# Half of the adjacency tiles built, the other half fetched as transposes

## The chip, the core and the metric

The kernel runs on one core of a Trainium2 chip. The core has a matrix engine (TensorE, PE in the profile; its weight loads are the row PEld), a vector engine (VectorE, DVE), an activation engine (ScalarE, ACT), a general engine (GpSimd, POOL) and a queue engine that issues transfers (SyncE, SP). ACT and POOL issue transfers too. All transfers of the core run on 16 DMA engines. The metric is device time in microseconds of one execution; lower is better.

## The reference, cut to what matters

A graph of N = 6250 nodes with 256 features has E = 106,250 directed edges: 50,000 drawn pairs in both directions and one loop for each node. The layer normalizes the features, runs two graph convolutions, adds a linear attention mix, and ends with a mixture of eight experts of which each node takes two. What the change touches is the aggregation inside the graph convolution:

```python
src = jnp.concatenate([edges[:, 0], edges[:, 1]])
dst = jnp.concatenate([edges[:, 1], edges[:, 0]])
deg = jax.ops.segment_sum(jnp.ones_like(dst, dtype=x.dtype), dst, num_segments=N_NODES)
deg = jnp.maximum(deg, 1.0)
agg = jax.ops.segment_sum(x[src], dst, num_segments=N_NODES) / deg[:, None]
return x @ W0 + b0 + agg @ W1 + b1
```

Every edge is taken in both directions, so the matrix A with agg = A x (before the division by the degree) is symmetric: A[u, v] counts the edges between u and v.

## The kernel before

The nodes are cut into NB = 49 blocks of P = 128. A is cut into 49 x 49 blocks of 128 x 128. The kernel treats T = 4 block columns at once as a group g; there are NGRP = 13 groups, the last one block wide. A *step* (g, j) handles the tile of A whose rows are block j and whose columns are the four blocks of group g: 128 x 512 elements, in bf16 128 KB. There are 13 x 49 = 637 steps, 49 of them narrow (128 x 128).

The kernel has five stages. The first (to about 383 us) normalizes the nodes and sorts edges into slots. The second, `aggregate` (the first graph pass, 383 to 1154 us), runs over all steps. The third, dense, stage (1154 to 1555 us) computes the first layer's output and the second layer's input. The fourth (the second graph pass, 1555 to 2192 us) multiplies by A again, and runs routing work (`gate`) of each finished group beside it. The fifth runs the experts.

A step of the first pass has these parts. `one_hots` (L649) compares slot numbers with a counter on DVE. `adjacency` multiplies two one-hot matrices for each of the blocks (L668), which gives the counts in PSUM, and copies them with ACT to a float tile `adj` (L671); the same instruction sums each row, which gives the degrees (`degp`). `keep` converts the tile to bf16 on DVE (L679) and stores it to DRAM (`adjd`, L680) from SP's queue. `products` multiplies (L626): the features of block j, split into a high and a low part (`sent`, k = 0 and 1), for two halves of the features (c), four matmuls of 512 columns, and adds into the two PSUM tiles `sum0` and `sum1` of the group over all j. The loop of `aggregate` runs these three out of step: comparisons for step t, building for step t - 1, storing and products for step t - 3. The order on PE, DVE and ACT is as written; in the first pass SP's is the scheduler's, which put stores in order of steps. `kept` and `adj` have four buffers each.

In the second pass `reload` (L808) reads seven steps' tiles in one transfer, with two buffers of seven steps; `widen` converts a tile from bf16 to float, by turns on ACT (L946) and DVE (L948), four steps ahead of `products`. The dense stage already issues the first two reloads. The scheduler decides SP's order in the second pass; the gate's load of `bt` (L956) is issued there too. Some expert weights are loaded from POOL's queue at the start of the second pass (L1093, L1095).

The dense stage's weights (`W0_0`, `W1_0`, `W0_1`, `W1_1`, 512 KB each) are loaded from POOL's queue ahead of the first pass (L608) and stay in memory through it.

`aggregate_any` is another way to compute the same, taken only where the edges don't fit the slots; here it is skipped.

Of the kernel before, what the change touches and what calls it, by code (L numbers as in the profile page):

```python
# [8 lines left out]
F32 = mybir.dt.float32  # L9
F32R = mybir.dt.float32r  # L10
BF16 = mybir.dt.bfloat16
I32 = mybir.dt.int32
AF = mybir.ActivationFunctionType
OP = mybir.AluOpType
AX = mybir.AxisListType
ENG = mybir.EngineType
PSUM = bass.MemoryType.PSUM
DRAM = bass.MemoryType.DRAM
P = 128

T = 4
# [18 lines left out]
def tile_gps_layer(ctx: ExitStack, tc: tile.TileContext, a, out):  # L40
    nc = tc.nc
# [9 lines left out]
    NB = -(-(N + 1) // P)  # L51
    NGRP = -(-NB // T)
# [14 lines left out]
    def blocks(g):  # L67
        return range(g * T, min(NB, g * T + T))
# [21 lines left out]
    adjd = dram.tile([NGRP, P, NB, T * P], BF16, name="adjd")  # L90
# [43 lines left out]
    with ExitStack() as p1:  # L134
# [153 lines left out]
        facts, hots, ranks = {}, {}, {}  # L288
# [284 lines left out]
        for b in range(NBAT):  # L573
            ahead_ = count(b + 1) if b + 1 < NBAT else iter(())
            k = b // (PK // PB) + 1
# [26 lines left out]
    wpool_ctx = tc.tile_pool(name="wgnn", bufs=1)  # L602
    wpool = wpool_ctx.__enter__()
    weights = {}
    for name in ("W0_0", "W1_0", "W0_1", "W1_1"):
        k, f = a[name].shape
        weights[name] = wpool.tile([P, k // P, f], F32, name="w" + name)
        nc.gpsimd.dma_start(weights[name], a[name].rearrange("(c p) f -> p c f", p=P))  # L608
    bh2 = wpool.tile([P, 2, FC], F32, name="bh2")
    nc.gpsimd.dma_start(bh2, a["bh"])  # L610
    bh = wpool.tile([P, FC], F32, name="bh")
# [4 lines left out]
    aggT = apool.tile([P, DC, NB * P], F32, name="aggT")  # L616
    degp = apool.tile([P, NB, NGRP], F32, name="degp")

    def products(pg, sums, adj, g, j):

        n = len(blocks(g))
        if j == 0:
            sums[g] = [pg.tile([P, T * P], F32, name=f"sum{c}") for c in range(DC)]
        for c in range(DC):
            for k in range(2):
                nc.tensor.matmul(sums[g][c][:, :n * P], sent[:, j, k, c * P:(c + 1) * P],  # L626
                                 adj[:, :n * P], start=(j == 0 and k == 0),
                                 stop=(j == NB - 1 and k == 1))

    steps = [(g, j) for g in range(NGRP) for j in range(NB)]  # L630

    def aggregate():

        with ExitStack() as s:
            hp = s.enter_context(tc.tile_pool(name="hots", bufs=4))
            ap = s.enter_context(tc.tile_pool(name="adj", bufs=4))
            pa = s.enter_context(tc.tile_pool(name="pa", bufs=4, space=PSUM))
            pg = s.enter_context(tc.tile_pool(name="pg", bufs=2, space=PSUM))
            s.enter_context(tc.manual_schedule(engines={ENG.PE, ENG.DVE, ENG.Activation}))
            hots, adjs, sums = {}, {}, {}  # L640

            def one_hots(t):
                g, j = steps[t]
                bs = blocks(g)
                n = len(bs)

                def compared(m, v0):
                    oh = hp.tile([P, m, P, 2], BF16, name=f"oh{m}")
                    nc.vector.tensor_tensor(  # L649
                        oh, iota2[:, None].to_broadcast([P, m, P, 2]),  # L650
                        place[:, j, v0:v0 + m, None, :].to_broadcast([P, m, P, 2]), op=OP.is_equal)
                    return oh

                hots[t] = (compared(n, bs[0]), compared(1, NB) if j in bs else None)

            def adjacency(t):
                g, j = steps[t]
                n = len(blocks(g))
                pt = pa.tile([P, T * P], F32, name="pt")
                oh, rest = hots.pop(t)  # L660
                for k, i in enumerate(blocks(g)):
                    cols = pt[:, k * P:(k + 1) * P]
                    if i == j:
                        todo = [(o, r) for o in (oh[:, k], rest[:, 0]) for r in range(2)]
                    else:
                        todo = [(oh[:, k], int(j > i))]
                    for m, (o, r) in enumerate(todo):
                        nc.tensor.matmul(cols, o[:, :, r], o[:, :, 1 - r], start=(m == 0),  # L668
                                         stop=(m + 1 == len(todo)))
                adj = ap.tile([P, T * P], F32R, name="adj")  # L670
                nc.scalar.activation(adj[:, :n * P], pt[:, :n * P], AF.Copy,  # L671
                                     accum_out=degp[:, j, g:g + 1])
                adjs[t] = adj

            def keep(t):
                g, j = steps[t]
                n = len(blocks(g))
                kept = ap.tile([P, T * P], BF16, name="kept")
                nc.vector.tensor_copy(kept[:, :n * P], adjs[t][:, :n * P].bitcast(F32))  # L679
                nc.sync.dma_start(adjd[g, :, j, :n * P], kept[:, :n * P])  # L680

            AH, AB = 3, 2
            for t in range(len(steps) + AH):
                if t < len(steps):
                    one_hots(t)
                if 0 <= t - AH + AB < len(steps):
                    adjacency(t - AH + AB)
                if t >= AH:
                    g, j = steps[t - AH]
                    keep(t - AH)  # L690
                    products(pg, sums, adjs.pop(t - AH), g, j)
                    if j == NB - 1:
                        n = len(blocks(g))
                        cols = slice(g * T * P, (g * T + n) * P)
                        nc.vector.tensor_copy(aggT[:, 0, cols], sums[g][0][:, :n * P])
                        nc.scalar.copy(aggT[:, 1, cols], sums[g][1][:, :n * P])

    def aggregate_any(first_conv):
# [3 lines left out]
        with tc.If(nc.values_load(misfit[0:1, 0:1], min_val=0, max_val=1) == 1), ExitStack() as s:  # L702
# [89 lines left out]
            if not first_conv:  # L792
                nc.vector.memset(rdeg, 0.0)

    aggregate()
    nc.vector.tensor_reduce(deg, degp, AX.X, OP.add)
    aggregate_any(True)
    ppool_ctx.__exit__(None, None, None)
    JL = 7
    lp_ctx = tc.tile_pool(name="reload", bufs=2, side="right")  # L800
    lp = lp_ctx.__enter__()
    loaded = {}

    def reload(t):
        g, j = steps[t]
        n = len(blocks(g))
        many = lp.tile([P, JL, T * P], BF16, name="many")
        nc.sync.dma_start(many[:, :, :n * P], adjd[g, :, j:j + JL, :n * P])  # L808
        loaded[g, j] = many


    with ExitStack() as p2:
# [4 lines left out]
        w = weights  # L817
        loads = {}

        def load_group(g):  # L820
            bs = blocks(g)
            cols = slice(bs[0] * P, (bs[-1] + 1) * P)
            xnT = wk.tile([P, DC, T * P], F32, name="xnT2")
            nc.sync.dma_start(xnT[:, :, :len(bs) * P], xnT_d[:, :, cols])
            loads[g] = xnT

        load_group(0)

        nc.vector.tensor_scalar(rdeg, deg, 1.0, None, op0=OP.max)
        nc.vector.reciprocal(rdeg, rdeg)  # L830
# [6 lines left out]
        for g in range(NGRP):  # L837
            bs = blocks(g)
            n = len(bs)
# [23 lines left out]
            for i, b in enumerate(bs):  # L863
                ts = slice(i * P, (i + 1) * P)
                pb = py.tile([P, 512], F32, name="pb")
                for c in range(DC):
                    nc.tensor.matmul(pb[:, :D], xnT[:, c, ts], wmix[:, c, :],
                                     start=(c == 0), stop=False)
                for f in range(FC):
                    nc.tensor.matmul(pb[:, :D], hT[f][:, ts], w["W0_1"][:, f, :], start=False,  # L870
                                     stop=(f == FC - 1))
                nc.vector.tensor_add(bt[:, i], bt[:, i], pb[:, :D])  # L872
                pz = py.tile([P, 512], F32, name="pz")
                for f in range(FC):
                    nc.tensor.matmul(pz[:, :D], hT[f][:, ts], w["W1_1"][:, f, :], start=(f == 0),
                                     stop=(f == FC - 1))
# [1 line left out]
                nc.vector.tensor_sub(sent[:, b, 1], pz[:, :D], sent[:, b, 0].bitcast(F32))  # L878
            nc.sync.dma_start(btab[cols, :].rearrange("(t p) d -> p t d", p=P), bt[:, :n])
            if g == 1:  # L880
                for t in range(0, 2 * JL, JL):
                    reload(t)

    apool_ctx.__exit__(None, None, None)
# [16 lines left out]
    first = gc.tile([P, T, NE], F32, name="first")  # L901
# [29 lines left out]
    with ExitStack() as p3:  # L931
        wk = p3.enter_context(tc.tile_pool(name="work3", bufs=2))
        ap = p3.enter_context(tc.tile_pool(name="adj2", bufs=5))
        pg = p3.enter_context(tc.tile_pool(name="pg2", bufs=2, space=PSUM))
# [3 lines left out]
        adjs, sums = {}, {}  # L938

        def widen(t):  # L940
            g, j = steps[t]
            n = len(blocks(g))
            adj = ap.tile([P, T * P], F32R, name="adj2")
            from_ = loaded[g, j - j % JL][:, j % JL, :n * P]
            if t % 2:
                nc.scalar.copy(adj[:, :n * P], from_)  # L946
            else:
                nc.vector.tensor_copy(adj[:, :n * P], from_)  # L948
            adjs[t] = adj
# [147 lines left out]
        AH = 4  # L1097
        running = iter(())
        for t in range(len(steps) + AH):
            if t < len(steps):  # L1100
                if steps[t][1] % JL == 0 and steps[t] not in loaded:
                    reload(t)
                widen(t)
            next(running, None)
            if t >= AH:
                g, j = steps[t - AH]
                products(pg, sums, adjs.pop(t - AH), g, j)
                if j == NB - 1:
                    for _ in running:
                        pass  # L1110
                    running = gate(g)
# [8 lines left out]
        for e in range(NE):  # L1120
# [35 lines left out]
                         stop=True)  # L1156
# [13 lines left out]
    with ExitStack() as p4:  # L1170
# [5 lines left out]
            engines={ENG.PE, ENG.DVE, ENG.Activation, ENG.SP, ENG.Pool}))  # L1176
# [147 lines left out]
```

## Time and profile before

| | |
|---|---|
| time, median of 3 runs | 2677.56 us (2676.61 to 2684.45) |
| the profiled execution's own time | 2674.58 us |
| its span, first to last instruction | 2672.8 us |
| granted TensorE clock, mean | 0.939 of full speed |
| first pass, busy | PE 768.9 of 771 us, DVE 633.7, ACT 428.3 |
| second pass, busy | PE 631.6 of 637 us, DVE 263.3, ACT 238.8 |
| SP's stores of tiles, L680 | 637, median 320 ns to issue each |

A profile row of the instruction groups names the line, the engine, the operation, the tile written and the tiles read, then the shapes and the count; then the busy time. In the timeline a row is: start, length, engine, line, operation, tiles; in brackets the idle time of that engine just before and what ended it. PE's matmuls overlap, so a step's length is read from one start to the next. A stretch row gives the busy time of each engine in that stretch, then the clock granted to TensorE, the mean busy share of the 16 DMA engines and their rate. The chain that ended last lies almost wholly in the experts' stage and says little of the passes; these are read from the stretches.

### The profile page before, as it was taken

How to read it: one execution, taken by the hardware profiler on the slowest of the kernel's cores; microseconds unless marked ns; L12 is line 12 of the kernel's file. 1: busy time of each engine (PE TensorE's matmuls, PEld its weight loads, DVE VectorE, ACT ScalarE, POOL GpSimd, SP SyncE). 2: the span in 40 equal slices, each digit the busy share in tenths (PEclk: the TensorE clock that was granted, in tenths of full speed). 3: DMA queues.
4: the chain of work that ended last, by engine and by line, in shares of the span. 5: the costliest groups of instructions: out<-in, count | busy, mean ns of one | idle time of the engine just before them, and what ended most of it. 6: DMA issues, size and time to landing. Idle time of an engine off the chain costs nothing. (4 is left out here: it accounts for less than half of the span.)

```text
span 2672.8 us, 41922 instructions
## 1 busy us (share of the span) xinstructions
PE 2452.5 (92%) x13030; PEld 1815.2 (68%) x13030; DVE 1587.8 (59%) x4247; ACT 951.0 (36%) x2476; POOL 344.6 (13%) x375
## 2 busy tenths in 40 slices
PE   3666769999999999989999989999999987999998
PEld 2455547777777777766677768888888874777665
DVE  5999888888888888721111124444434434666665
ACT  1332225555555555511111123334334322323332
POOL 0000000000000000000000011121121122454444
PEclk7777779999999999979999989999999978999999
DMA  2111613333333333222111154445454433223333
GB/s 75 52 51 52 209 54 109 108 107 107 107 107 107 105 110 108 86 66 83 55 56 55 50 208 150 165 161 168 156 166 162 150 120 96 77 76 103 105 112 96
DMA packets 227535, 286.75 MB, mean 107 GB/s; under 512 B 51798, under 2 KB 199937, under 8 KB 227046
## 3 DMA queue, kind: packets, MB, share of 16 engines
q1 hardware_dynamic: 204386, 241.06, 28.1%
q0 software_dynamic: 17072, 34.33, 3.8%
q10 hardware_dynamic: 5844, 8.58, 0.9%
q8 instruction: 107, 1.75, 0.3%
q14 instruction: 126, 1.03, 0.1%
HBM read 151.43 MB, written 147.10 MB: 112 GB/s over the span
## 5 line engine op out<-in xcount | busy, mean ns | idle before, releaser
L626 PE MATMUL sum<-adj,sent 128*128 128x512 f32 (+1 forms) x5096 | 1332.4, 403 | 10.2 <-DVE blank L918 5.9
L626 PEld LDWEIGHTS sum<-adj,sent 128*128 128x128 f32 x5096 | 907.9, 196 | 161.4 <-issue 6.3
L671 ACT ACTIVATE adj<-pt 128x512 fp32r<-128x512 f32 (+1 forms) x637 | 365.7, 574 | 337.2 <-PE pt L668 335.8
L649 DVE TENSOR_TENSOR oh<-iota,place 128x1024 bf16<-128x1024 bf16 (+1 forms) x686 | 426.7, 628 | 0.3 <-PE pt L668 0.2
L679 DVE CAST kept<-adj 128x512 bf16<-128x512 f32 (+1 forms) x637 | 262.1, 411 | 114.9 <-ACT adj L671 106.6
L946 ACT CAST adj<-many 128x512 fp32r<-128x512 bf16 (+1 forms) x318 | 188.8, 595 | 385.9 <-PE sum L626 345.1
L948 DVE CAST adj<-many 128x512 fp32r<-128x512 bf16 (+1 forms) x319 | 135.8, 427 | 318.2 <-PE sum L626 254.8
L668 PE MATMUL pt<-oh 128*128 128x128 bf16 x2548 | 261.5, 224 | 2.4 <-DVE oh L649 1.8
L668 PEld LDWEIGHTS <-oh 128*128 128x128 bf16 x2548 | 151.1, 99 | 161.8 <-DVE oh L649 131.3
L1226 PEld LDWEIGHTS po<-w2e,hT 128*128 128x128 f32 x840 | 159.4, 190 | 67.3 <-issue 26.3
L1206 PE MATMUL pm<-w1e,yT 128*128 x420 | 200.2, 599 | 1.8 <-DMA row<-lists 1.3
L1226 PE MATMUL po<-w2e,hT 128*128 x840 | 198.5, 379 | 1.0 <-ACT hT L1218 1.0
L1230 ACT ACTIVATE res<-res,row 128x256 f32<-128x256 f32 x105 | 53.3, 508 | 301.3 <-DVE res L1229 152.0
L453 PE MATMUL rt<-carry,route 128*128 128x100 bf16 x931 | 81.8, 265 | 84.5 <-DVE carry L440 65.3
L907 POOL IOTA home_i<- 128x8 int32 x1 | 0.1, 128 | 1158.5 <-DVEq L702 1158.5
L453 PEld LDWEIGHTS <-route 128*128 128x128 bf16 x931 | 73.1, 132 | 94.7 <-issue 84.5
L1085 POOL DMA_INDIRECT lists<-rows,place_i x98 | 97.2, 991 | 298.5 <-DVE rows L1077 265.1
L1262 POOL DMA_INDIRECT out_dram<-both,at x105 | 106.0, 1009 | 161.5 <-DVE both L1260 158.7
L872 DVE TENSOR_TENSOR bt<-bt,pb 128x256 f32<-128x256 f32 x49 | 20.6, 421 | 174.1 <-PE pb L870 174.1
L671 ACT ACTIVATION_READ_ACCUMULATOR adj<-pt 128x1 f32 x637 | 123.9, 194 | 0.0
L1247 POOL DMA_INDIRECT got<-ybuf,at x105 | 108.1, 1030 | 84.5 <-issue 33.0
L1209 DVE TENSOR_TENSOR hb<-pm,b1c 128x512 f32<-128x512 f32 x105 | 72.7, 692 | 64.2 <-PE pm L1206 62.0
(253 smaller groups left out, 2557.4 us busy)
## 6 DMA issues: line engine op xcount, KB each, us to landing
adjd<-kept SPq DMA_DIRECT2D x588, 128.0 KB
many<-adjd SPq DMA_DIRECT2D x84, 896.0 KB
row<-lists SPq DMA_DIRECT2D x105, 130.5 KB
ybuf<-xn SPq DMA_DIRECT2D x1, 13440.0 KB
ybuf<-res SPq DMA_DIRECT2D x105, 128.0 KB
xn<-in_x_dram SPq DMA_DIRECT2D x12, 512.0 KB
xnT_d<-xnT ACTq DMA_DIRECT2D x12, 512.0 KB
xnT<-xnT_d SPq DMA_DIRECT2D x12, 512.0 KB
```

The lines of the kernel that those rows point to most:

```text
L453: nc.tensor.matmul(pl[:, r], routes[q // 4][:, q % 4, :, r], carry[:, q - q0, :, :, r], start=(q == 0), stop=(q == Q - 1))
L626: nc.tensor.matmul(sums[g][c][:, :n * P], sent[:, j, k, c * P:(c + 1) * P], adj[:, :n * P], start=(j == 0 and k == 0), stop=(j == NB - 1 a ...
L649: nc.vector.tensor_tensor(oh, iota2[:, None].to_broadcast([P, m, P, 2]), place[:, j, v0:v0 + m, None, :].to_broadcast([P, m, P, 2]), op=OP ...
L668: nc.tensor.matmul(cols, o[:, :, r], o[:, :, 1 - r], start=(m == 0), stop=(m + 1 == len(todo)))
L671: nc.scalar.activation(adj[:, :n * P], pt[:, :n * P], AF.Copy, accum_out=degp[:, j, g:g + 1])
L679: nc.vector.tensor_copy(kept[:, :n * P], adjs[t][:, :n * P].bitcast(F32))
L946: nc.scalar.copy(adj[:, :n * P], from_)
L948: nc.vector.tensor_copy(adj[:, :n * P], from_)
L1206: nc.tensor.matmul(pm, yT[:, c], w1e[:, bass.ds(e, 1), c, :].rearrange("p o f -> p (o f)"), start=(c == 0), stop=(c == DC - 1))
L1226: nc.tensor.matmul(po, hT[:, f], w2e[:, bass.ds(e, 1), f, :].rearrange("p o d -> p (o d)"), start=(f == 0), stop=(f == EC - 1))
L1247: ga = nc.gpsimd.indirect_dma_start(out=gots[t % 4], out_offset=None, in_=ybuf, in_offset=bass.IndirectOffsetOnAxis(ap=outs[t][1][:, 0:1], ...
L1262: st = nc.gpsimd.indirect_dma_start(out=out, out_offset=bass.IndirectOffsetOnAxis(ap=at[:, 1:2], axis=0), in_=both, in_offset=None, bounds ...
```

## The change

Only tiles with j >= 4g (on and below the diagonal in a group's numbering) are built. A tile with j < 4g is "turned": its four blocks are fetched as transposes of blocks that earlier groups stored. For four j at once (j to j + 3, all in group j // 4) and each block i of group g, one transfer on SP's queue reads 128 x 512 elements of bf16, the stored tile of step (j // 4, i), and writes four transposed blocks. So four such transfers (one in the last group) make the tiles of four steps. The steps of a group are put in another order: first the built j from 4g to 48, then the turned ones from 0.

In the first pass a turned step has no comparisons, no building matmuls, no cast and no store; ACT's instruction remains and reads the fetched bf16 tile instead of PSUM. The turned tiles have three buffers of four steps (`turned`), and are asked for eight steps ahead of the products; the one-hot tiles have three buffers instead of four. SP's order is as written there now. In the second pass nothing of the loop's engines changes but the reload: tiles come four steps at a time with three buffers, eight steps ahead, built ones by a plain transfer and turned ones by the transposing transfers, which are made again. The dense stage issues the first two reloads (eight steps). `W0_1` and `W1_1` are loaded at the start of the dense stage from ACT's queue.

```diff
+    def load_weights(pool, queue, *names):
+        for name in names:
+            k, f = a[name].shape
+            weights[name] = pool.tile([P, k // P, f], F32, name="w" + name)
+            queue.dma_start(weights[name], a[name].rearrange("(c p) f -> p c f", p=P))
+
+    load_weights(wpool, nc.gpsimd, "W0_0", "W1_0")
...
-    steps = [(g, j) for g in range(NGRP) for j in range(NB)]
+    steps = [(g, j) for g in range(NGRP) for j in (*range(g * T, NB), *range(g * T))]
+
+    def is_turned(t):
+        g, j = steps[t]
+        return j < g * T
+
+    def ends_of(g):
+
+        return g * T, (g * T - 1) % NB
+
+    def turn_tiles(pool, g, j):
+
+        tl = pool.tile([P, T, T, P], BF16, name="some")
+        for k, i in enumerate(blocks(g)):
+            nc.sync.dma_start(tl[:, :, k, :], adjd[j // T, :, i, :], transpose=True)
+        return tl.rearrange("p j k q -> p j (k q)")
...
-            hp = s.enter_context(tc.tile_pool(name="hots", bufs=4))
+            hp = s.enter_context(tc.tile_pool(name="hots", bufs=3))
             ap = s.enter_context(tc.tile_pool(name="adj", bufs=4))
+            tp_ = s.enter_context(tc.tile_pool(name="turned", bufs=3))
...
-            s.enter_context(tc.manual_schedule(engines={ENG.PE, ENG.DVE, ENG.Activation}))
+            s.enter_context(tc.manual_schedule(engines={ENG.PE, ENG.DVE, ENG.Activation, ENG.SP}))
...
+                adj = ap.tile([P, T * P], F32R, name="adj")
+                adjs[t] = adj
+                if is_turned(t):
+                    nc.scalar.activation(adj[:, :n * P], turned[g, j - j % T][:, j % T, :n * P],
+                                         AF.Copy, accum_out=degp[:, j, g:g + 1])
+                    return
...
-            AH, AB = 3, 2
-            for t in range(len(steps) + AH):
-                if t < len(steps):
+            AT, AH, AB = 8, 3, 2
+            for t in range(AH - AT, len(steps) + AH):
+                if (a_ := t + AT - AH) < len(steps) and is_turned(a_) and steps[a_][1] % T == 0:
+                    turned[steps[a_]] = turn_tiles(tp_, *steps[a_])
+                if 0 <= t < len(steps) and not is_turned(t):
                     one_hots(t)
                 if 0 <= t - AH + AB < len(steps):
                     adjacency(t - AH + AB)
                 if t >= AH:
                     g, j = steps[t - AH]
-                    keep(t - AH)
-                    products(pg, sums, adjs.pop(t - AH), g, j)
-                    if j == NB - 1:
+                    if not is_turned(t - AH):
+                        keep(t - AH)
+                    first, last = ends_of(g)
+                    products(pg, sums, adjs.pop(t - AH), g, j, j == first, j == last)
+                    if j == last:
...
-    JL = 7
-    lp_ctx = tc.tile_pool(name="reload", bufs=2, side="right")
+    lp_ctx = tc.tile_pool(name="reload", bufs=3, side="right")
...
+    AR = 8
...
+        if j % T:
+            return
+        if is_turned(t):
+            loaded[g, j] = turn_tiles(lp, g, j)
+        else:
+            n, m = len(blocks(g)), min(T, NB - j)
+            some = lp.tile([P, T, T, P], BF16, name="some").rearrange("p j k q -> p j (k q)")
+            nc.sync.dma_start(some[:, :m, :n * P], adjd[g, :, j:j + m, :n * P])
+            loaded[g, j] = some
...
         load_group(0)
+        load_weights(p2.enter_context(tc.tile_pool(name="wgnn2", bufs=1)), nc.scalar, "W0_1", "W1_1")
...
-                for t in range(0, 2 * JL, JL):
+                for t in range(AR):
                     reload(t)
...
-                if steps[t][1] % JL == 0 and steps[t] not in loaded:
-                    reload(t)
+                reload(t + AR)
                 widen(t)
```

More of the change, by code (lines that the diff above doesn't have):

```diff
@@ L604, in tile_gps_layer @@
     weights = {}
[L605 to L608, printed above, removed]
+    def load_weights(pool, queue, *names):
[4 more added lines that the diff above has]
+    load_weights(wpool, nc.gpsimd, "W0_0", "W1_0")
     bh2 = wpool.tile([P, 2, FC], F32, name="bh2")
@@ L617, in tile_gps_layer, with products @@
     degp = apool.tile([P, NB, NGRP], F32, name="degp")
-    def products(pg, sums, adj, g, j):
+    def products(pg, sums, adj, g, j, first, last):
         n = len(blocks(g))
-        if j == 0:
+        if first:
             sums[g] = [pg.tile([P, T * P], F32, name=f"sum{c}") for c in range(DC)]
@@ L626, in products @@
                 nc.tensor.matmul(sums[g][c][:, :n * P], sent[:, j, k, c * P:(c + 1) * P],
-                                 adj[:, :n * P], start=(j == 0 and k == 0),
-                                 stop=(j == NB - 1 and k == 1))
-    steps = [(g, j) for g in range(NGRP) for j in range(NB)]
+                                 adj[:, :n * P], start=(first and k == 0),
+                                 stop=(last and k == 1))
+    steps = [(g, j) for g in range(NGRP) for j in (*range(g * T, NB), *range(g * T))]
[9 more added lines that the diff above has]
+        return tl.rearrange("p j k q -> p j (k q)")
     def aggregate():
         with ExitStack() as s:
-            hp = s.enter_context(tc.tile_pool(name="hots", bufs=4))
+            hp = s.enter_context(tc.tile_pool(name="hots", bufs=3))
             ap = s.enter_context(tc.tile_pool(name="adj", bufs=4))
+            tp_ = s.enter_context(tc.tile_pool(name="turned", bufs=3))
             pa = s.enter_context(tc.tile_pool(name="pa", bufs=4, space=PSUM))
             pg = s.enter_context(tc.tile_pool(name="pg", bufs=2, space=PSUM))
-            s.enter_context(tc.manual_schedule(engines={ENG.PE, ENG.DVE, ENG.Activation}))
-            hots, adjs, sums = {}, {}, {}
+            s.enter_context(tc.manual_schedule(engines={ENG.PE, ENG.DVE, ENG.Activation, ENG.SP}))
+            hots, adjs, sums, turned = {}, {}, {}, {}
             def one_hots(t):
@@ L669, in adjacency @@
                                          stop=(m + 1 == len(todo)))
-                adj = ap.tile([P, T * P], F32R, name="adj")
                 nc.scalar.activation(adj[:, :n * P], pt[:, :n * P], AF.Copy,
                                      accum_out=degp[:, j, g:g + 1])
-                adjs[t] = adj
             def keep(t):
@@ L798, in tile_gps_layer @@
     ppool_ctx.__exit__(None, None, None)
-    JL = 7
-    lp_ctx = tc.tile_pool(name="reload", bufs=2, side="right")
+    lp_ctx = tc.tile_pool(name="reload", bufs=3, side="right")
     lp = lp_ctx.__enter__()
     loaded = {}
+    AR = 8
     def reload(t):
+        if t >= len(steps):
+            return
         g, j = steps[t]
[L806 to L809, printed above, removed]
+        if j % T:
+            return
+        if is_turned(t):
[5 more added lines that the diff above has]
+            loaded[g, j] = some
     with ExitStack() as p2:
@@ L943, in widen @@
             adj = ap.tile([P, T * P], F32R, name="adj2")
-            from_ = loaded[g, j - j % JL][:, j % JL, :n * P]
+            from_ = loaded[g, j - j % T][:, j % T, :n * P]
             if t % 2:
@@ L1106, in tile_gps_layer @@
                 g, j = steps[t - AH]
-                products(pg, sums, adjs.pop(t - AH), g, j)
-                if j == NB - 1:
+                first_, last = ends_of(g)
+                products(pg, sums, adjs.pop(t - AH), g, j, j == first_, j == last)
+                if j == last:
                     for _ in running:
```

## The prediction

> **What bounds the kernel now.** The page first, for the totals, then busy time and granted clock by stage, then one step of each graph pass in order of time.
>
> The head of the page and its engine rows:
>
> ```profile
> span 2672.8 us, 41922 instructions
> PE 2452.5 (92%) x13030; PEld 1815.2 (68%) x13030; DVE 1587.8 (59%) x4247; ACT 951.0 (36%) x2476; POOL 344.6 (13%) x375
> ```
>
> Stretches of the trace: first pass, second pass (columns: length, then busy time and count of PE, PEld, DVE, ACT, POOL, then granted clock, DMA share, GB/s):
>
> ```profile
> 383.00:1154.00 771.00, 768.86 (x5095) 558.70 (x5096) 633.71 (x1337) 428.28 (x1288) 4.28 (x6) 0.98 0.32 106
> 1555.00:2192.00 637.00, 631.59 (x2956) 516.11 (x2956) 263.29 (x946) 238.84 (x399) 116.50 (x140) 0.97 0.49 162
> ```
>
> PE is busy from end to end in both, at nearly the full clock; DVE has 137 us free in the first, SP and DMA more. One built step of the first pass:
>
> ```profile
> 702.95 0.40 PE L668 MATMUL pt<-oh 128*128 128x128 bf16 x4
> 703.16 1.17 PE L626 MATMUL sum<-adj,sent 128*128 128x512 f32 x4
> 703.24 0.69 DVE L649 TENSOR_TENSOR oh<-iota,place 128x1024 bf16<-128x1024 bf16 x1
> 703.35 0.32 SPq L680 DMA_DIRECT2D adjd<-kept  x1
> 703.39 0.60 ACT L671 ACTIVATE adj<-pt 128x512 fp32r<-128x512 f32 x1 [0.53 <-PE pt L668]
> 703.88 0.19 ACT L671 ACTIVATION_READ_ACCUMULATOR adj<-pt 128x1 f32 x1
> 704.11 0.43 DVE L679 CAST kept<-adj 128x512 bf16<-128x512 f32 x1 [0.19 <-ACT adj L671]
> 704.17 0.40 PE L668 MATMUL pt<-oh 128*128 128x128 bf16 x4
> ```
>
> The step repeats after 704.17 - 702.95 = 1.22 us. The same products without building, from ACT's conversions in the second pass (every second step is ACT's):
>
> ```profile
> 1801.70 0.62 ACT L946 CAST adj<-many 128x512 fp32r<-128x512 bf16 x1 [1.25 <-PE sum L626]
> 1803.56 0.62 ACT L946 CAST adj<-many 128x512 fp32r<-128x512 bf16 x1 [1.25 <-issue]
> ```
>
> 1.86 us for two steps, 0.933 a step. So building a tile costs the path 1.22 - 0.933 = 0.287 us; PE hides the rest.
>
> **What is removed.** Of 13 x 49 = 637 steps, group g turns 4g: 4 x (0+...+12) = 312. Of these 264 (g up to 11) are four blocks wide, 48 (g = 12) one block. Wide: 264 x 0.287 = 75.8 us. The narrow ones run at half clock in the trace:
>
> ```profile
> 1134.00:1136.00 2.00, 2.00 (x12) 2.00 (x12) 0.86 (x4) 0.76 (x6) 0.00 (x0) 0.50 0.15 33
> ```
>
> 12 matmuls in 2 us are 0.167 us each; the built step has five, the turned one four: 48 x 0.167 = 8.0 us. Together **84 us off**, all in the first pass; the second multiplies what it did before. With them go 312 comparisons and casts on DVE and 312 stores on SP, none on the path; ACT keeps its instruction and degree read (0.62 + 0.19 = 0.81 us, under 0.933).
>
> **What is added: 552 transposing transfers on SP.** 66 wide turned groups of four transfers and 12 narrow ones of one make 276 in each pass, each 128 x 512 bf16, 128 KB. Four feed four steps, and the first step needs all four, because each brings one block for every j. PE takes 4 x 0.933 = 3.73 us for these steps, so a transfer is hidden if SP and the DMA engines pass one each 0.933 us. The trace has no such operation. Bounds:
>
> - From below, data alone. The narrow stores just shown move 256-byte rows at 33 GB/s with a DMA share of 0.15, or 220 GB/s at full share: 131,072 B take 0.60 us. The Trainium skill ("DMA: Bandwidth & Descriptors", Latency and other measured facts) gives 261 GB/s for a DMA transpose with a non-contiguous middle dimension: 0.50 us. Either hides it: the sum is **-84 us**.
> - Against the change speaks the skill's "VectorE: DVE Perf Modes" (The three transpose paths): a 128 x 128 bf16 transpose by DMA takes 1309 ns, and its rules prefer TensorE where PSUM will do. The row beside it here is four built blocks for 0.287 us on PE. At the rate of 261 GB/s the data of one such block are 0.125 us, so about 1.2 us is fixed. If SP is held for it, a transfer costs about 1.31 us whatever its size up to ours, four take 5.24 us, and every group of four steps is 5.24 - 3.73 = 1.51 us late.
> - From above, four blocks one after the other: 4 x 1.309 = 5.2 us, far from both rates.
>
> The nearest plain load, a 130.5 KB one in the final chain, lands 1.85 us after issue, yet SP issues a plain one in 0.32 us: whether a transpose's fixed time is passed in the background or holds SP is the open point. I take 1.31 us as held, since it is the only price for the operation itself.
>
> **How much of the lateness shows.** Three buffers let the first group of a phase start nine steps ahead, 9 x 0.933 = 8.4 us; it uses 5.24 and an estimated 1.5 us to land, leaving 1.7 us. A phase of g groups ends (g-1) x 1.51 - 1.7 us late: over g = 3..11, 1.51 x 54 - 9 x 1.7 = 66 us a pass. The phases of g = 9, 10, 11 have only 13, 9 and 5 plain steps before them and cannot regain the whole lead: I add 11 (with no lead anywhere it would be 66 x 1.51 = 100). In the first pass the stores of 12 built tiles (0.32 us each) stand between the first transfers on SP: 5 more. So **+82 us in the first pass, +77 in the second**. In the first, stores wait on SP behind transposes, the four `kept` buffers fill, DVE's cast waits and the next comparisons with it, but comparisons are not needed in a turned phase. ACT waits for the tile, PE for ACT. In the second pass ACT's and DVE's conversions wait and the gate's work behind them; its `bt` load stands on SP among the transposes.
>
> **Does the clock fall while PE waits?** A late transfer in the second pass of before shows the price:
>
> ```profile
> 1574.18 8.07 PE L626 MATMUL sum<-adj,sent 128*128 128x512 f32 x23 [3.92 <-DVE adj L948]
> ...
> 1575.00:1580.00 5.00, 5.00 (x14) 3.84 (x13) 0.43 (x1) 0.91 (x2) 0.00 (x0) 0.54 1.02 427
> 1580.00:1585.00 5.00, 5.00 (x23) 4.05 (x22) 1.28 (x3) 1.57 (x3) 0.00 (x0) 1.00 0.53 192
> ```
>
> After 3.92 us idle the clock was 0.54 for some 5 us, and 14 matmuls ran where 23 do. "TensorE: Matmul & The Clock Gate" (Why this matters for your kernels) sets the limit at idle gaps over about 3 us; waits of 1.51 us in 5.24 would cost nothing. But the trace fell to 0.50 near 1125 us after a gap of 1.04 us among narrow matmuls[...]. A cold group needs 16 x 0.427 = 6.8 us instead of 5.24; if all 132 wide groups were cold, that adds 206 us. PE would then be fully busy, which brought the clock back above. I count 0 and keep 206 in the range.
>
> **Small parts.** W0_1 and W1_1 (1 MB) load at the start of the dense stage on ACT's queue; L870 needs them at 1179.2 us, 21 us after the stage's first load at 1157.9; at the first pass's 106 GB/s for a share of 0.32, 331 GB/s, they take 3.2 us: nothing; uncovered, 3.2 us. The second pass starts with 8 steps in hand instead of 14, beside expert weights that keep the DMA share at 1.02 until 1580; the 3.92 us stall grows by up to the missing 6 x 0.933 = 5.6 us: +5. The order of products within a group costs nothing.
>
> **Sum.** -84 + 82 + 77 + 5 = +80 us. The profiled execution took 2674.58 us (span 2672.8 and 1.8 around it); plus 80 is 2754.6. The median of the runs shown is 3 us above that execution, within their spread of 8; I say **2756 us**.
>
> **Rivals.** *Hidden transfers:* SP is free again early, as with 0.32 us for a plain issue, and the data need 0.5 to 0.6 us. For it: DMA share only 0.32 and 0.49, both rates. Against it: 1309 ns for one block. It decides below about 0.95 us a transfer. Time: 2677.6 - 84 + 5 = 2599 us. *Issue and data add up:* 1.18 fixed + 0.50 us of data, 1.69 us each, four 6.76, 3.03 late a group; a phase then has no spare at all (6.76 + 1.5 against 8.4), so 66 x 3.03 = 200 us a pass: 2677.6 - 84 + 400 + 5 = 2999 us. For it: the operation may not overlap itself on one queue; against it: plain transfers do. *Four blocks in turn:* 5.2 us, four 20.8, 17.1 late: 132 x 17.1 = 2257 us, so 4856 us; the page's 261 GB/s contradicts it. *The clock falls:* 1.31 us and cold groups, up to 2756 + 206 = 2962 us. That fewer tiles are turned than planned is excluded by the steps above.
>
> **How the numbers follow.** 1.31 us held, warm or partly cold: 0.50 (2670 to 2860 us, for 1.15 to 1.5 us a transfer; at about 1.15 it breaks even, so a small part of this case is faster or the same). Hidden: 0.24. Added up or mostly cold: 0.22. Four in turn: 0.04. Faster by over 0.3%: 0.24 + 0.04 = 0.28; within 0.3%, about what a measurement of this kernel can tell: 0.03; slower: 0.69. The range 2588 to 2990 leaves out the worst of the last two cases, some 0.2.
>
> **What would show it.** PE's matmuls of the building line fall from 2548 to 1444 (264 x 4 + 48 fewer), and a fully covered turned step in the first pass takes 0.93 us. Right: transposing issues on SP about 1.3 us each and back to back in the turned phases, ACT waiting for `some`, waits growing with g. Wrong: issues near 0.3 us, ACT waiting for PE in turned phases, the first pass near 690 us; or a spacing of 1.7 us and more; or the clock at half in turned phases.

## The result and the profile after

The changed kernel takes 2763.33 us (median of 4 runs, 2757.11 to 2773.99) against 2677.09 us before (4 runs, 2675.91 to 2684.45): a ratio of 1.032, 95% interval 1.0283 to 1.0357. It is slower by 3.2%; the forecast was 2756 us. The profiled execution took 2757.11 us, 82.5 us more than that of before.

The head of its page:

```profile
span 2755.3 us, 38946 instructions
PE 2416.9 (88%) x11926; PEld 1788.2 (65%) x11926; DVE 1312.8 (48%) x3623; ACT 937.9 (34%) x2476; POOL 345.1 (13%) x373
```

PE has 36 us less to do and the span is 82 us longer: PE waits now. Where, the stretches of its trace for the two passes tell (length, then busy time and count of PE, PEld, DVE, ACT, POOL, then clock, DMA share, GB/s):

```profile
383.00:1160.00 777.00, 702.33 (x3976) 517.23 (x3973) 360.48 (x707) 416.54 (x1284) 0.60 (x2) 0.97 0.39 104
1560.00:2270.00 710.00, 652.23 (x2927) 522.42 (x2928) 258.64 (x957) 235.64 (x398) 114.53 (x138) 0.95 0.54 145
```

PE is idle for 75 us in the first pass and for 58 in the second, where it was idle for 2 and 5. The view of waits names who waits (engine, line, waited for, us in total, times, longest):

```profile
DVE adj L986 <- DMA some<-adjd: 204.6, 63, 7.7
ACT adj L984 <- DMA some<-adjd: 194.4, 59, 6.6
...
ACT adj L683 <- DMA some<-adjd: 158.9, 51, 5.0
```

L683 reads the turned tile in the first pass, L984 and L986 widen in the second; both wait for fetched tiles. The issuing instruction itself, from the view of its line (durations in ns, lowest, median and highest, then the starts of the first and the last):

```profile
L650 SPq DMA_TRANSPOSE some<-adjd x552: 935/1264/2395, 488.6 to 2262.3; - x184
```

This operation, of which the kernel before had none, holds SP for 1264 ns, where a plain issue held it for 320. One turned phase (g = 4, sixteen turned steps) in order of time on SP:

```profile
655.90 5.12 SPq L650 DMA_TRANSPOSE some<-adjd  x4
661.12 1.99 SPq L705 DMA_DIRECT2D adjd<-kept  x4
663.19 5.12 SPq L650 DMA_TRANSPOSE some<-adjd  x4
668.41 1.98 SPq L705 DMA_DIRECT2D adjd<-kept  x4
670.48 10.35 SPq L650 DMA_TRANSPOSE some<-adjd  x8
```

Four transposes take 5.12 us and follow each other without a gap; the products of four steps take 3.73. Between the first groups stand stores of tiles, four at a time. What SP itself waits for, from the view of its queue's waits:

```profile
SPq L705 <- DVE kept L704: 251.6, 237, 10.2
```

The stores wait for DVE's casts, and in SP's written order a transpose behind such a store waits with it.

By stage, read from the starts of the first and last product matmul in each pass (us); the last column is the first experiment:

| | before | after | one wide transfer |
|---|---|---|---|
| up to the first product | 385.6 | 383.2 | 385.3 |
| first pass | 768.4 | 776.6 | 673.2 |
| between | 401.1 | 402.7 | 403.0 |
| second pass | 636.4 | 713.5 | 639.2 |
| after the last product | 481.3 | 479.3 | 479.5 |
| span | 2672.8 | 2755.3 | 2580.2 |

### The profile page after: what moved, and what is told of

Read it like the earlier page. It is cut to its first block, busy times and chain, and to the rows that moved or that the text cites. A ratio compares the mean times of both kernels' runs of the same rounds, so it can differ in the third digit from the quotient of the medians.

```text
span 2755.3 us, 38946 instructions
## 1 busy us (share of the span) xinstructions
PE 2416.9 (88%) x11926; PEld 1788.2 (65%) x11926; DVE 1312.8 (48%) x3623; ACT 937.9 (34%) x2476; POOL 345.1 (13%) x373
## 5 line engine op out<-in xcount | busy, mean ns | idle before, releaser
L630 PE MATMUL sum<-adj,sent 128*128 128x512 f32 (+1 forms) x5096 | 1306.0, 405 | 119.2 <-ACT adj L683 74.3
L984 ACT CAST adj<-some 128x512 fp32r<-128x512 bf16 (+1 forms) x318 | 184.6, 594 | 462.7 <-PE sum L630 227.3
L986 DVE CAST adj<-some 128x512 fp32r<-128x512 bf16 (+1 forms) x319 | 132.8, 423 | 400.2 <-DMA some<-adjd 204.6
L697 ACT ACTIVATE adj<-pt 128x512 fp32r<-128x512 f32 (+1 forms) x325 | 194.3, 598 | 177.6 <-PE pt L695 176.2
L683 ACT ACTIVATE adj<-some 128x512 fp32r<-128x512 bf16 (+1 forms) x312 | 178.1, 572 | 179.1 <-DMA some<-adjd 158.9
L670 DVE TENSOR_TENSOR oh<-iota,place 128x1024 bf16<-128x1024 bf16 (+1 forms) x374 | 231.5, 634 | 14.9 <-PE pt L695 0.2
L704 DVE CAST kept<-adj 128x512 bf16<-128x512 f32 (+1 forms) x325 | 137.5, 424 | 36.8 <-DMA adjd<-kept 25.9
L695 PEld LDWEIGHTS <-oh 128*128 128x128 bf16 x1444 | 84.5, 99 | 88.3 <-DVE oh L670 61.2
L695 PE MATMUL pt<-oh 128*128 128x128 bf16 x1444 | 141.2, 224 | 0.6 <-DVE misfit L599 0.6
L1244 PEld LDWEIGHTS pm<-w1e,yT 128*128 128x128 f32 x420 | 72.6, 193 | 54.4 <-issue 52.7
```

The source lines that it names most:

```text
L670: nc.vector.tensor_tensor(oh, iota2[:, None].to_broadcast([P, m, P, 2]), place[:, j, v0:v0 + m, None, :].to_broadcast([P, m, P, 2]), op=OP ...
L683: nc.scalar.activation(adj[:, :n * P], turned[g, j - j % T][:, j % T, :n * P], AF.Copy, accum_out=degp[:, j, g:g + 1])
L1244: nc.tensor.matmul(pm, yT[:, c], w1e[:, bass.ds(e, 1), c, :].rearrange("p o f -> p (o f)"), start=(c == 0), stop=(c == DC - 1))
```

## The experiments

The theory was that SP is held for each transposing transfer, that four in a row cannot keep up with the products, and that without this hold the transfers are hidden in both passes. Rivals were the bytes in the DMA engines, and the order, the lead and the smaller parts of the change. Edits are shown against the changed kernel.

**One wide transfer in place of four.**

```diff
-        for k, i in enumerate(blocks(g)):
-            nc.sync.dma_start(tl[:, :, k, :], adjd[j // T, :, i, :], transpose=True)
-        return tl.rearrange("p j k q -> p j (k q)")
+        bs = blocks(g)
+        nc.sync.dma_start(tl.rearrange("p a b q -> p (a b) q")[:, :len(bs) * T, :],
+                          adjd[j // T, :, bs[0]:bs[-1] + 1, :].rearrange("p i c -> p (i c)"),
+                          transpose=True)
+        return tl.rearrange("p k j q -> p j k q")
```

The two readers of the tile take it as `[P, n, 128]`, in pieces of 128 columns.

> One transposing transfer of 128 x 2048 (512 KB) takes the place of the four of 128 x 512 in every wide turned group; the bytes are the same, the turned tile lies in another order in memory and ACT and DVE read it in pieces of 128 columns. Theory (SP is held about 1.26 us for a transfer because of what it does for each transfer, not for the bytes): one transfer holds SP at most half as long as the four together (under 2.6 us against 5.1), a group is hidden behind 3.73 us of products, both passes lose their lateness: 2677 - 84 - 10 (narrow steps at full clock) = about 2585 us. Rival (the hold is the bytes passing the DMA engines, 128 KB in 1.26 us): one transfer holds SP about 5.1 us and the time stays near 2760 us.

Measured: 2582.27 us (4 runs, 2580.54 to 2584.25), 0.9663 of before (0.9633 to 0.9694). It is faster than both kernels: 3.4% below before. Its transposing line, and its two passes:

```profile
L650 SPq DMA_TRANSPOSE some<-adjd x156: 1188/1956/4504, 490.7 to 2087.0; - x156
```

```profile
383.00:1058.00 675.00, 674.84 (x3987) 510.99 (x3988) 362.77 (x712) 436.22 (x1286) 2.96 (x4) 1.00 0.45 119
...
1462.00:2101.00 639.00, 633.48 (x2956) 519.74 (x2954) 263.58 (x943) 240.14 (x399) 115.62 (x139) 0.97 0.60 161
```

The same 512 KB hold SP for 1.96 us instead of 5.12, and PE is busy throughout both passes again. The DMA share goes up to 0.45 and 0.60, at 119 and 161 GB/s: the engines had room for these bytes all along. The rival of the bytes is out.

**Plain copies in the transposes' place.** This kernel leaves the transposing out, so its turned tiles hold untransposed blocks and its output is not the layer's; only its time is of use.

```diff
-            nc.sync.dma_start(tl[:, :, k, :], adjd[j // T, :, i, :], transpose=True)
+            nc.sync.dma_start(tl[:, :, k, :], adjd[j // T, :, i, :].rearrange("p (j q) -> p j q", q=P))
```

> The four transfers of every wide turned group are kept in number, bytes and place, but they copy the stored blocks as they are and do not transpose them (so the turned tiles hold untransposed blocks). Theory (the transposing operation itself holds SP): a copy holds SP 0.32 us, the waits for turned tiles vanish in both passes, about 2585 us. Rival (order of steps, three buffers, eight steps ahead or stores in front of the loads cause the waits): near 2760 us still.

Measured: 2581.06 us (4 runs), 0.9655 of before (0.9624 to 0.9685), passes of 673.0 and 639.8 us. The issuing line:

```profile
L650 SPq DMA_DIRECT2D some<-adjd x552: 359/505/1579, 488.9 to 2085.9; - x184
```

552 transfers of the same bytes at the same places in the program, median 0.505 us each, and nothing waits. So neither the number of transfers nor their place costs anything; what costs is that they transpose, and the wide transfer shows that it counts how often.

**Nothing turned, all else kept.**

```diff
     def is_turned(t):
-        g, j = steps[t]
-        return j < g * T
+        return False
```

> Nothing is turned: all tiles are built as before, but the order of steps in a group, the buffers, the reload of four steps with eight in hand, and the late load of W0_1 and W1_1 are those of the changed kernel. Prediction's small parts: 2677 + 5 = 2682 us, with the 5 at the start of the second pass. Rival (these parts carry a good share of the loss): over 2700 us.

Measured: 2671.54 us (12 runs), 0.9993 of before (0.9975 to 1.0012): no difference. Order, buffers and late weights cost nothing together. The second pass is 3.2 us longer than before's (639.6), the first 1.9 shorter. The expectation of 2682 us was too high: the 5 us at the start of the second pass did not come.

**Stores from POOL's queue.**

```diff
-                nc.sync.dma_start(adjd[g, :, j, :n * P], kept[:, :n * P])
+                nc.gpsimd.dma_start(adjd[g, :, j, :n * P], kept[:, :n * P])
```

> The changed kernel with the stores of built tiles issued from POOL's queue, so that SP holds only transposing transfers in the first pass. Theory (stores stand between the first transfers of a phase, each waiting in turn behind 5.1 us of transposes and for DVE's casts): each phase from g = 3 on starts its third group 4 us earlier, 9 x 4 = 36 us less in the first pass, nothing in the second: about 2727 us. Rival (the stores fit into gaps and only the transposes' throughput counts): within 8 us of 2760.

Measured: 2698.91 us (4 runs), 1.011 of before (1.0075 to 1.0145); first pass 704.2 us against 776.6. The gain is there, but it is 72 us, twice what was expected. (The second pass is 6.7 us longer, 720.2 against 713.5; a wait of 8.5 us in its first group accounts for it, and why it is there was not looked into.) SP in that kernel begins:

```profile
394.31 231.34 SPq L650 DMA_TRANSPOSE some<-adjd  x36
```

The first transpose starts at 394 us, where the changed kernel starts it at 489: with no stores in front, SP fetches as soon as the source tiles are in DRAM and a buffer is free, so in most phases three groups lie ready when the turned steps begin. Lateness then shows from g = 6 on only (groups last 54.8 us at g = 5, 54.0 at 6, 57.3 at 11; with the wide transfer 54.8, 53.6 and 47.2).

**Asked for twelve steps ahead.**

```diff
-            AT, AH, AB = 8, 3, 2
+            AT, AH, AB = 12, 3, 2
```

> The changed kernel with its turned tiles asked for twelve instead of eight steps ahead of the products in the first pass; buffers, transfers and stores stay as they are and the stores stay on SP. Theory (SP's written order puts the first three groups of each phase behind stores that wait for DVE, so they start too late): the three start four steps of 1.22 us earlier, 4.9 us less for each phase from g = 3 to 11, 44 us in all: first pass 777 - 44 = 733 us, whole about 2719 us. Rival (stores cost because each takes 0.32 to 0.5 us of SP, or because their bytes slow the transposes, wherever they stand): first pass within 10 us of 777, whole near 2760 us.

Measured: 2738.81 us (4 runs), 1.0246 of before (1.0211 to 1.028); first pass 751.9 us, 25 less, where 44 were expected by the theory and none by its rival. Each had half. SP in the phase g = 4:

```profile
645.72 5.82 SPq L650 DMA_TRANSPOSE some<-adjd  x4
651.64 1.98 SPq L705 DMA_DIRECT2D adjd<-kept  x4
653.71 5.12 SPq L650 DMA_TRANSPOSE some<-adjd  x4
658.93 1.99 SPq L705 DMA_DIRECT2D adjd<-kept  x4
661.02 5.11 SPq L650 DMA_TRANSPOSE some<-adjd  x4
666.23 1.98 SPq L705 DMA_DIRECT2D adjd<-kept  x4
668.30 5.12 SPq L650 DMA_TRANSPOSE some<-adjd  x4
```

SP's first transposes start 10 us earlier here, but now three sets of stores stand among the transposes instead of two. A set takes 2.07 us (653.71 - 651.64). The third set is there in the phases g = 4 to 9 alone, so it costs about 12 us. By stages, the turned phases of the first pass are 34 us shorter together than in the changed kernel, and the phases of built steps 9.5 us longer; what makes these longer was not tested. So stores on SP cost in two ways: they hold the first transposes back, and they take the queue while it is the bottleneck. How the 72 us divide between the two is not settled: two sets in each of nine phases would be 37 us, and the rest is then left for the first.

**Halves and pairs: what the hold depends on.** In the first, each transfer of the second pass alone is cut in two; in the second, each wide group uses two transfers of two blocks in the layout of the wide one.

```diff
-            nc.sync.dma_start(tl[:, :, k, :], adjd[j // T, :, i, :], transpose=True)
+            for h in range(0, T, w := T // parts):
+                nc.sync.dma_start(tl[:, h:h + w, k, :], adjd[j // T, :, i, h * P:(h + w) * P],
+                                  transpose=True)
...
+        for k in range(0, len(bs), 2):
+            m = min(2, len(bs) - k)
+            nc.sync.dma_start(tl.rearrange("p a b q -> p (a b) q")[:, k * T:(k + m) * T, :],
+                              adjd[j // T, :, bs[k]:bs[k] + m, :].rearrange("p i c -> p (i c)"),
+                              transpose=True)
```

> In the second pass alone every transposing transfer is cut in two of 128 x 256 (64 KB each): eight instead of four for a group, the same bytes. The first pass stays as in the changed kernel. Theory (a fixed hold of about 1.2 us for each transfer up to 128 KB): eight take about 9.8 us against 3.73 us of products, 6.1 late for 66 groups, less a little lead: about 400 us over the hidden second pass of 639 us, so 1040 us, and the whole about 3080 us. Rival (hold in proportion to bytes, 0.63 us for 64 KB): the second pass stays at 714 us, the whole near 2760 us.

Measured: 3081.61 us (one run; before 2676.66 on the same chip), second pass 1035.4 us.

> Two transposing transfers of 128 x 1024 (256 KB) for each wide turned group, laid out as in the one of 128 x 2048. Between 1.26 us for 128 KB and 1.96 us for 512 KB lie two readings. Hold growing evenly with bytes: 1.5 us for 256 KB. Flat up to 256 KB and growing after: 1.2 to 1.3 us. By both, two take 2.5 to 3.0 us, under 3.73: no waits, about 2585 us.

Measured: 2580.2 us (one run), passes of 673.9 and 635.7 us. The lines of the two, halves (which include the first pass's uncut transfers) and then pairs:

```profile
L651 SPq DMA_TRANSPOSE some<-adjd x828: 1167/1244/2517, 488.6 to 2588.1; - x166
```

```profile
L652 SPq DMA_TRANSPOSE some<-adjd x288: 1188/1269/3099, 490.7 to 2083.1; - x144
```

SP's hold is 1.24 us for 64 KB, 1.26 for 128, 1.27 for 256, and 1.96 for 512: flat from 64 to 256 KB, and longer at 512. The even growth with bytes is out, and the halves cost what the fixed hold says, 1035 us where 1040 were expected. The contiguous rows in DRAM grow with the size, from 512 bytes to 4 KB; the two were not varied apart.

## Why the prediction was right, and where its terms were not

The mechanism was right: SP is held for each transposing transfer, and four in a row are slower than the products. That the sum came out within 3 us of the measured one is in part luck: the narrow steps saved 10 us more than forecast, and the first pass was late by 21 us more.

| term of the sum | predicted | measured | from |
|---|---|---|---|
| building saved, wide steps | -75.8 | -76.8 | groups 0 to 11, wide transfer less before |
| building saved, narrow steps | -8.0 | -18.5 | last group, 22.6 less 41.1 |
| late in the first pass | +82 | +103.4 | 776.6 less 673.2 |
| late in the second pass | +77 | +74.3 | 713.5 less 639.2 |
| second pass with nothing late (forecast for its start) | +5 | +2.8 | 639.2 less 636.4 |
| the rest | 0 | -2.7 | stages outside the passes, after less before |
| sum | +80 | +82.5 | |

**What is removed.** Right for the wide steps, and the building matmuls went from 2548 to 1444 as forecast. The narrow steps were costed at the half clock at which the kernel before ran them. After, the last group enters at the full clock and keeps it:

```profile
1142.00:1146.00 4.00, 4.00 (x38) 4.00 (x37) 0.00 (x0) 3.38 (x21) 0.00 (x0) 1.00 0.39 89
```

38 matmuls in 4 us are 0.105 us each instead of 0.167. The kernel before fell to 0.50 right after PE had waited for a comparison on DVE, which a turned step does not have:

```profile
1125.61 0.29 PE L668 MATMUL pt<-oh 128*128 128x128 bf16 x1 [1.04 <-DVE oh L649]
```

The step that failed was to carry the clock of a row over to steps without the wait that stood in front of it. The nine traces agree with this. Their last groups in the two passes make 18 narrow stretches: in eleven PE had a gap of 0.38 to 1.04 us, and the clock fell to half within 8 us of it; in seven there was no gap over 0.25 us, and it stayed at full. The kernel with nothing turned is among the eleven (0.78 us in the first pass). No run changes the gap alone, so this is an agreement of traces and not a test.

**The price of a transfer.** Right. Held are 1.26 us, and two in a row start 1.308 us apart (median of the 232 starts in the first pass that follow another within 1.6 us), so a group takes 5.23 us. From the last issue of a late group to ACT's first instruction on it pass 1.6 us, where 1.5 were estimated. The row of the Trainium skill's "VectorE: DVE Perf Modes" (The three transpose paths), 1309 ns for a block of 128 x 128, came out as the spacing at four such blocks. The prediction took it over to our size because it had no other price, and not for a reason; that the hold is nearly the same from 64 to 256 KB only the runs show, and none has a transfer of a single block. The rate of 261 GB/s of "DMA: Bandwidth & Descriptors" (Latency and other measured facts) does not describe our transfers of 128 KB, where SP passes 100 GB/s. At 512 KB, 524,288 B in the 1.956 us of the hold are 268 GB/s, near to it; whether that is the case which the page measured no run here shows.

**How much shows.** The second pass came out at 74.3 for 77, with the growth that was forecast: its turned phases are late by 2.1 us at g = 2, by 3.5 to 8.5 at g = 3 to 9, and by 14.5 and 13.3 at g = 10 and 11. In the first pass, 103 for 82 hides two errors that cancelled in part. Without stores on SP the lateness was put at 77 us, for a lead of nine steps; with the stores out of the way three whole groups are ready ahead, and it is only 31.0 us (704.2 less 673.2). And the stores on SP, put at 5 us, cost 72.4 us (776.6 less 704.2). The term that was mis-sized is "the stores of 12 built tiles (0.32 us each)". These are 12 x 0.32 = 3.8 us in each phase, about 35 us in nine phases, and the sum took them about once. It also counted their issue alone, not that a transpose behind them cannot start before DVE has made their tiles, nor that a set of four takes 2.07 us of the queue that is late. That `kept` fills and DVE's cast waits was seen as predicted (L704 waits 25.9 us for its stores), and it delayed little that PE needed: the first pass's phases of built steps are 1.2 us longer in all than with one wide transfer.

**The start of the second pass.** The 5 us did not come: its first group takes 53.1 us, and 54.2 before. The 2.8 us of the wide transfer's row stand at the other end, in the last, narrow group, which takes 42.8 us there and 37.7 before, with the clock falling to half at different times in it. In the changed kernel it takes 38.4, so that the 74.3 us of that row are 77.4 in the wide turned phases, less 4.4 here and plus 1.4 elsewhere.

**The clock.** Counted at 0, with 206 us kept in the range. The trace has short dips inside the turned phases, here in the second pass:

```profile
1968.00:1972.00 4.00, 2.93 (x13) 1.92 (x13) 1.32 (x7) 2.62 (x4) 0.00 (x0) 1.00 0.44 98
1972.00:1976.00 4.00, 1.80 (x5) 1.49 (x5) 1.60 (x8) 0.62 (x1) 0.00 (x0) 0.63 0.44 99
1976.00:1980.00 4.00, 4.00 (x11) 3.08 (x10) 1.12 (x6) 0.89 (x2) 0.00 (x0) 0.52 0.44 100
1980.00:1984.00 4.00, 4.00 (x19) 3.24 (x18) 0.86 (x6) 0.97 (x2) 1.28 (x2) 1.00 0.47 105
```

In eight microseconds with 4.7 us of PE work the clock fell, and after about 7 us at half it was back. The mean clock of the passes went from 0.98 and 0.97 to 0.97 and 0.95. Eighteen such dips lie in the turned phases of the two passes. Each follows, within 10 us, a wait of PE of 1.6 to 3.6 us; none follows shorter waits alone. So the even waits of 1.51 us were harmless, as the prediction had it. But the first waits of a phase are longer, and ten of the dips follow waits under the 3 us that the prediction took as the limit, while some waits of that length are followed by none. For the same products PE is busy 27 us longer in the first pass and 19 in the second than with one wide transfer (674.8 and 633.5 us). What this costs was not measured apart; while SP sets the pace, a slower matmul fills time in which PE would wait, and the phases of built steps, where SP does not, are longer by 1.2 and 1.4 us alone.

**The rivals.** Hidden transfers (2599 us) is what one wide transfer makes true at 2582: the bytes were never the limit. Its sign, a hold of about 0.3 us, was not there. Issue and data adding up to 1.69 us fell with the 1.26 us measured, four blocks in turn likewise.

## What to carry to other kernels

A transfer that has a fixed hold on its issuing queue is costed as queue time: so many instructions in the phase times the hold, against the time of the work that it has to keep up with, and the first cure is fewer and larger transfers. A queue that is late should not also carry instructions that wait for another engine; what stands in front of its first transfers costs again in every phase, and has to be counted once for each. A price quoted for one size says nothing about another until it is known whether it is the fixed part or the bytes.

## What the runs showed of the hardware

A transposing transfer of bf16 from DRAM held SP for 1.24 to 1.27 us from 64 KB to 256 KB and for 1.96 us at 512 KB, while plain transfers held it for 0.32 to 0.5 us. Because of the flat part the rate of the queue grew with the size of a transfer: 100 GB/s at 128 KB, with starts 1.308 us apart, and 268 at 512 KB by the hold. A group of narrow matmuls, 128 columns each, took 22.6 us at the full clock, where PE had no gap in it (steps of four matmuls), and 41.1 us where the clock was at half after a gap of 1.04 us (steps of five). Among 512-column matmuls the clock dipped to half for 3 to 7 us after waits of 1.6 to 3.6 us.
